# The product h*c moved to VectorE, and three smaller edits, in a conv-attention-LSTM kernel

## The chip, the cores and the metric

The kernel runs on one core of a Trainium2 chip. The metric is device microseconds of one execution. Five engines work side by side, each with its own queue in a fixed order: TensorE (PE; PEld is its weight load), VectorE (DVE), ScalarE (ACT), GpSimd (POOL), and SyncE (SP), which here issues DMAs alone.

## The reference

Eight images of 56 x 56 x 256 go through two layers, all in float32. In short:

```
x = x + conv_attn(group_norm(x))      # 7x7 regions of 64 tokens; each region attends to the 4 regions
                                      # that its pooled query ranks highest; of 256 keys the best 32
                                      # scores of each query are kept (k2 = TS // 8); plus a 3x3 depthwise
                                      # convolution of v, plus an output projection
t = x as (8, 3136, 256)
t = t + window_attn(layer_norm(t))    # each token attends to 3 neighbours on either side
xt = layer_norm(t);  h = c = 0
for step in range(3136):              # a recurrence over the tokens, 8 images at once
    i = sigmoid(xt @ U_i + b_i + h @ V_i);   g = tanh(xt @ U_c + b_c + h @ V_c)
    o = sigmoid(xt @ U_o + b_o + h @ V_o)
    c = h * c + i * g                 # the old h takes the place of a forget gate
    h = o * tanh(c)
t = t + all h
```

The product that the change moves is `h * c` in the line of the new c.

## The kernel before

**Stages.** An image is cut into 7 rows of 448 tokens (`ROW`, 7 regions of 64). A unit is one row of one image; the 56 units run row by row, and within a row over the 8 images. A unit does `queries_and_lepe` (projections and convolution), 7 times `region` (attention of one region), `project`, and `window_attention`, whose last part, `gates`, writes the terms xt @ U + b of the recurrence to DRAM (`xgd`). Ahead of that, `norm_and_route` reads each image twice: once for statistics, once for keys and values. In what follows all of this is called the bulk work.

**The recurrence** (`recurrence`, lines 1304 to 1411) can take a row's 448 tokens once all eight images have finished that row. So the tokens of row p run beside the bulk work of row p+1, and the tokens of the last row run alone, at the end. A step of the recurrence is a chain over four engines:

- `sums_of`: 24 small matmuls add h @ V to a PSUM bank (`r_sum`) that already holds the token's terms;
- ACT: tanh of the bank to `r_th` (the sigmoids are tanhs of halved arguments);
- DVE: a 32 x 32 block transpose of `r_th` into `cell`, a buffer in which the gates and the old product stand interleaved (there are two, used in turn);
- DVE: `tensor_tensor_scan` over `cell` gives the new c (`r_c`), and reads i, g and the product h*c there;
- ACT: tanh of c to `r_tc`; DVE: `scalar_tensor_tensor` of the output gate and `r_tc` gives h, in `r_hs`.

Beside the chain, ACT halves c (`r_half`, line 1375), POOL multiplies it by h into the cell of the next step (line 1377), and an empty instruction on DVE (`seen_by`, line 314) waits for that product. From token 2688 on (`APART`), the output gate has matmuls, tanh and transpose of its own, and only 16 matmuls stand in the chain.

Terms come from DRAM by `load_terms`: `XB` tokens at a time, in four DMAs each, into two buffers `r_gin`; `place` copies two tokens' terms to a PSUM bank on ACT.

**The planner.** `_Plan` records every operation with an estimate of how long it holds its engine (`held`) and when its result is there (`late`), from `_time` or `timed`; then `run` (line 369) plays all five engines forward, chooses for each engine the ready operation of the lowest rank, and so fixes the order of every queue. Operations of the recurrence have rank 0 and `chain=True`, or rank -1 for those beside it. Bulk work may start only if it ends by `until`, the time at which the chain is expected on that engine plus a slack. For DVE this is `max(20, 1.5 * (due - now))` ns past the due time (line 434). A long operation of POOL is held back in part of each step (line 438). When PE would idle for over `FILL` ns ahead of its next work, a matmul of no use (`spare`, line 641) is put in, which keeps PE busy.

**Two-operand operations on POOL.** Over 400 ns and with two tensors each are: `pe - left` in `region` (line 983, 28 in a unit), the bias of the gates (1212, 12 in a unit), the biases of `project` and `window_attention` (1056 and 1155, 4 each), and the sum of a region (1020, 7 in a unit).

**Normalisations.** `normalize` (785) works on `xn` (two operations in a unit) and on `xchunk` (`keys_values`, two in each of 56 calls); `layer_norm` (1027) on `xln`, twice for each block of 112 tokens. All are `tensor_scalar` on DVE: subtract a mean, multiply by a scale.

Of the kernel before, what the change touches and what calls it, by code (L numbers as in the profile page):

```python
# [10 lines left out]
F32 = mybir.dt.float32  # L11
# [29 lines left out]
TB = 16  # L41
XB = 8
GATES = 3
# [15 lines left out]
FAR = 10**12  # L59
FILL = 250  # L60
LONG = 400
SLACK = {"PE": 60, "DVE": 120, "ACT": 60, "POOL": 60, "SP": 1000}

# [39 lines left out]
def _time(engine, name, view, reads, args, kw):  # L103

    n = max([_count(v) for v in [view] + reads])
    if engine == "SP":
        return 650, 2400 + 9 * n // 4
    if engine == "PE":
        held = 160 if name == "transpose" else 5 * _count(view) // 3 + 110
        return held, held + 200  # L110
    if engine == "POOL":
        t = 180 + 15 * n // 7
        return (1050, 1050) if ALU.pow in args else (t + 90, t)
    if engine == "ACT":
        t = 5 * n // 7 + 100
        if kw.get("accum_out") is not None:
            return t + 150, t + 260
        if isinstance(kw.get("bias"), _View) or view.buf.banks:
            return t + 120, t + 200
        return t + 20, t + 110  # L120
    held = 25 * n // 24 + 60
    if name == "reciprocal":
        return 20 * n // 3 + 60, 20 * n // 3 + 150
    if name == "transpose":
        return held + 40, held + 120
    if name == "tensor_tensor_scan":
        return 2 * n + 80, 2 * n + 170
    if name == "match_replace":
        return held + 65, held + 150
    if name == "scalar_tensor_tensor":  # L130
        return held + 20, held + 100
    return held, held + 90
# [72 lines left out]
class _Op:  # L205
    __slots__ = (
        "engine", "trace", "held", "late", "rank", "chain", "before", "open", "due", "start",
        "takes", "pair", "made",
    )
# [24 lines left out]
class _Plan:  # L234
# [78 lines left out]

    def seen_by(self, engine, op, view):


        def trace():
            made = engine.engine.engine_nop()
            self.tc.add_manual_dep(
                made.ins, op.made[0].ins.name,  # L320
                mybir.DependencyInfo(mybir.DependencyClass.Sync, mybir.DependencyReason.DATA),
                reason="seen before it is read",
            )

        self.add(engine.name, [trace], [view], [], 10, 10)
        return self.ops[-1]

    def add(self, engine, traces, reads, writes, held, late):
        op = _Op()
        op.engine, op.trace, op.held, op.late = engine, traces, held, late  # L330
        op.rank, op.chain = self.mode
        op.rank = (op.rank, len(self.ops))
        op.before, op.takes, op.start = {}, [], None
        op.pair = engine == "DVE" and len(reads) > 1
        self.ops.append(op)
        for views, write in ((reads, False), (writes, True)):
            for v in views:
                self._depend(op, v, write)
                if v.buf.pool is not None:
                    if not v.buf.users:  # L340
                        op.takes.append(v.buf)
                    if not v.buf.users or v.buf.users[-1] is not op:
                        v.buf.users.append(op)
# [25 lines left out]
    def run(self, tc, fill):  # L369
# [35 lines left out]
        def expected(engine):  # L405
# [3 lines left out]
            for k in range(at, min(at + 7, len(chain))):  # L409
# [8 lines left out]
                if op.engine == engine or engine == "POOL" and op.pair:  # L418
                    return t
            return FAR  # L420

        filled = tied = 0
        while len(done) < len(ops) + filled:
            moved = False
            for e in engines:
# [7 lines left out]
                due = expected(e)  # L433
                until = due + (SLACK[e] if e != 'DVE' else max(20, 1.5 * (due - now)))
                for i, (rank, op) in enumerate(ready[e]):
                    if not op.chain and now + op.held > until:
                        continue
                    if e == "POOL" and op.held > LONG and (at % 6 > 3 or tied < at // 6):

                        continue  # L440
                    if any(b.free and not self._room(b, made, now) for b in op.takes):
                        continue
                    del ready[e][i]
                    op.start = now
                    free[e] = now + op.held
                    heappush(events, free[e])
                    heappush(events, now + op.late + HOP)
# [4 lines left out]
                    for b, gap in op.before.items():  # L452
                        b.due = max(b.due, now + gap)
                        b.open -= 1
                        if not b.open:
                            opened(b)
                    if op.chain:
                        at += 1
                    elif e == "POOL" and op.rank[0] == 0:
                        tied += 1  # L460
# [13 lines left out]
            if not moved:  # L474
# [4 lines left out]
                now = heappop(events)  # L479
        self.length = now  # L480
        with tc.manual_schedule():
            for op in done:
                for t in op.trace:
                    t()

    def _room(self, buf, made, now):
# [23 lines left out]
def _layers(ctx: ExitStack, tc, a, out):  # L510
# [146 lines left out]
    hss = [nc.fixed(t, (P, 2, TB, SLOT)) for t in hss]  # L657
    state = {"seen": None, "h": hss[1][:, :, TB - 1].as_of(hss[1][:, :, TB - 1, LAST:])}
    t2, xg = [], []
# [10 lines left out]
    def norm_and_route(b, im):  # L670
# [22 lines left out]
        def groups():  # L693
# [16 lines left out]
            im["rs"] = rs = images_p.tile([P, 2], F32, name="grs")  # L710
            _rsqrt(nc, rs, gm[:, 1, :], 1e-5, mhalf[:, 0:2])

        def route():
# [71 lines left out]
    def normalize(im, t):  # L785
        for k in range(2):
            nc.vector.tensor_scalar(
                t[:, k, :], t[:, k, :], im["gm"][:, 0, k : k + 1], im["rs"][:, k : k + 1],
                ALU.subtract, ALU.mult,
            )  # L790
# [109 lines left out]
    def region(qi, unit, im, row):  # L900
# [35 lines left out]
        for pair in range(groups // 2):  # L936
            both = ps_sc.tile([P, 2, 512], F32, name="sc")
            with nc.rank(0.5), nc.together(600, 800):
                for g2 in range(2):
# [86 lines left out]

    def layer_norm(i, src, mv, rs, nq=QB):

        xl = two.tile([QB, C], F32, name="xln")
        nc.vector.tensor_scalar(  # L1030
            xl[:nq], src, mv[:nq, i, 0:1], rs[:nq, i : i + 1], ALU.subtract, ALU.mult
        )
# [7 lines left out]
    def project(b, unit, im, row):  # L1040
# [30 lines left out]
        def end():  # L1071
# [3 lines left out]
            )  # L1075
            rs = small.tile([QB, NQB], F32, name="rs")
            _rsqrt(nc, rs[:, :nblk], mv[:, :nblk, 1], 1e-5, mhalf[:QB, :nblk])
            for i in range(nblk):
                nc.scalar.copy(
                    xc[:, :, LEAD + i * QB : LEAD + (i + 1) * QB],  # L1080
                    layer_norm(i, x1[:, i, :], mv, rs),
                )
# [14 lines left out]
    def window_attention(b, unit, im, row):  # L1097
# [88 lines left out]
        def begin_gates():  # L1186
            blocks = len(sizes)
            row["rs2"] = small.tile([QB, NQB + 1], F32, name="rs2")
            _rsqrt(
                nc, row["rs2"][:, :blocks], row["mv2"][:, :blocks, 1], 1e-5,  # L1190
                mhalf[:QB, :blocks],
            )
            for i, q in enumerate(sizes):
                nc.sync.dma_start(t2[t0 // QB + i][:, b, :], row["t2"][:q, i, :])

        def gates(i):
            q = sizes[i]
            xl = two.tile([P, 2, QB], F32, name="xlT")[:, :, :q]
            nc.scalar.copy(
                xl, layer_norm(i, row["t2"][:q, i, :], row["mv2"], row["rs2"], q)  # L1200
            )
# [98 lines left out]
    def blocks(t):  # L1300

        return t.rearrange("p (k g b) -> p k g b", k=2, b=nb)

    def recurrence(blk):

# [11 lines left out]
        def step(t):  # L1317
# [4 lines left out]
            now = slice(at % 2 * UJ, (at % 2 + 1) * UJ)  # L1322
            cell, after = cells[at % 2], cells[(at + 1) % 2]
            gates = cell[:, 2 : 2 + 4 * CELL].rearrange(
# [4 lines left out]
            if at < APART:  # L1329
                with nc.rank(0, chain=True):  # L1330
# [3 lines left out]
                    nc.timed(150, 190)  # L1334
                    nc.vector.transpose(gates, blocks(th))
            else:

# [18 lines left out]
            with nc.rank(0, chain=True):  # L1356
# [10 lines left out]
                nc.timed(130, 187)  # L1367
                if state["seen"]:
                    nc._edge(state["seen"], nc.ops[-2], False)
                hn = hs[:, :, t, LAST:]  # L1370
                nc.vector.scalar_tensor_tensor(hn, out_gate, 1.0, tch, ALU.add, ALU.mult)
                nc.timed(92, 161)
            state["h"] = hs[:, :, t].as_of(hn)
            half = rwork.tile([P, 2, nb], F32, name="r_half")
            nc.scalar.activation(half, c[:, :, :, 2], AF.Copy, scale=0.5)
            hc = after[:, CELL + 2 : 2 * CELL + 2].rearrange("p (k b e) -> p k b e", b=nb, e=3)
            nc.gpsimd.tensor_tensor(hc[:, :, :, 2], hn, half, ALU.mult)
            with nc.rank(-1):
                state["seen"] = nc.seen_by(nc.vector, nc.ops[-1], hc[:, :, :, 2])
            if at < APART:  # L1380
# [81 lines left out]
    for s in after(len(units) - 1):  # L1462
        s()
    made["tokens"] = SHIFTED
    follow(ready, -(-SHIFTED // TB))
# [69 lines left out]
```

## Time and profile before

| | |
|---|---|
| median of 3 runs | 9221.27 us (9216.84 to 9227.03) |
| profiled execution | 9223.24 us |
| its span | 9221.5 us |
| granted TensorE clock, mean | 0.989 |
| busy: PE, PEld | 93%, 62% |
| busy: DVE, ACT, POOL | 84%, 61%, 35% |
| first, last update of r_c | 1350.0 us, 9215.6 us |
| matmuls of no use (`spare`) | 1699.7 us |

A busy share is that of an engine over the whole span; matmuls overlap one another, so PE's is not a share of its peak. Nearly every operation is issued from one line of the recorder (L302), so groups are told apart by tile names: `r_` names belong to the recurrence. In the lists of groups, the first number behind the bar is the busy time of the group in us, the second the mean of one instruction in ns.

The run has three parts. Up to 1350 us there is bulk work alone; from there to 8300 us the bulk work and six rows of the recurrence run side by side; from 8300 us the last 451 tokens run alone.

### The profile page before, as it was taken

Reading aid. Unit: us, or ns where it says so; the run is one execution under the profiler, and the core shown is the slowest. Engines: PE = TensorE matmul, PEld = TensorE weight load, DVE = VectorE, ACT = ScalarE, POOL = GpSimd, SP = SyncE. Lnnn points to the kernel's source line nnn. Section 1 sums busy time; section 2 is a strip of 40 time slices with the busy share of each in tenths; the row PEclk is TensorE's granted clock in tenths of the full one; section 3 lists DMA queues with packets and bytes.
Section 4 is the critical chain, followed back from the end, with each engine's and each line's share of the span. In section 5 each row is a group of like instructions: output and inputs, shape, how many; then the busy total and the mean of one; then the engine's idle time right before and its main releaser. Section 6 shows DMA issues by size and latency. Waiting matters only on the chain.

```text
span 9221.5 us, 494813 instructions
## 1 busy us (share of the span) xinstructions
PE 8606.6 (93%) x200866; PEld 5694.5 (62%) x200866; DVE 7734.8 (84%) x32968; ACT 5612.8 (61%) x22855; POOL 3249.4 (35%) x7747
## 2 busy tenths in 40 slices
PE   7989989999999999999999999999999999999999
PEld 4555556666566666666656666566665666657887
DVE  6787899899999999989998899989999988864444
ACT  3555556666666666666666666666666666654444
POOL 1232343343433434333343333433334343331111
PEclk9999999999999999999999999999999999999999
DMA  6545432323323333332333323333233323220000
GB/s 198 153 130 161 112 104 79 88 79 92 89 79 88 80 90 87 81 87 77 93 82 84 89 77 89 83 87 90 78 89 81 89 75 83 76 64 25 25 24 22
DMA packets 1071250, 798.03 MB, mean 87 GB/s; under 512 B 402366, under 2 KB 1001524, under 8 KB 1068964
## 3 DMA queue, kind: packets, MB, share of 16 engines
q1 hardware_dynamic: 1068964, 766.36, 31.0%
q8 instruction: 1580, 25.89, 1.2%
q14 instruction: 706, 5.78, 0.2%
HBM read 527.08 MB, written 238.88 MB: 83 GB/s over the span
## 4 chain that ended last, share of the span: by engine, by line
DVE 50%; PE 28%; ACT 6%; issue 3%; DMA 2%; POOL 0%; SPq 0%; DVEq 0%; POOLq 0%; ACTq 0%
DVE left L302 15%; PE r_sum L302 13%; DVE top L302 13%; PE mm L302 9%; DVE r_c L302 7%; DVE r_cell L302 5%; DVE r_hs L302 4%; ACT r_th L302 2%; PE spare L641 2%; PE pt_av L302 2%; ACT r_tc L302 1%; PE sc L302 1%; DVE st L302 1%; DVE xln L302 1%; DMA xn<-xh 1%
## 5 line engine op out<-in xcount | busy, mean ns | idle before, releaser
L302 PE MATMUL r_sum<-r_v,r_hs 128*8 128x64 f32 (+2 forms) x150528 | 2715.8, 220 | 353.1 <-DVE r_hs L302 234.4
L302 PEld LDWEIGHTS r_sum<-r_v,r_hs 128*8 128x8 f32 (+2 forms) x150528 | 2180.1, 96 | 1285.8 <-DVE r_hs L302 1190.5
L302 POOL TENSOR_TENSOR r_cell<-r_hs,r_half 128x16 f32<-128x16 f32 x3136 | 714.3, 228 | 3999.7 <-DVE r_hs L302 2679.3
L302 DVE MATCH_REPLACE8 left<-top,left 128x256 f32<-128x256 f32 x4704 | 1901.9, 408 | 0.0
L302 DVE MAX8 top<-left 128x8 f32<-128x256 f32 x4704 | 1852.1, 412 | 1.9
L302 ACT ACTIVATE r_th<-r_sum 128x64 f32<-128x64 f32 x3587 | 797.9, 222 | 1679.1 <-PE r_sum L302 1633.9
L641 PE MATMUL spare<-ident 128*32 128x128 f32 x11852 | 1699.7, 277 | 9.8 <-issue 8.2
L302 DVE STREAM_TRANSPOSE r_cell<-r_th 128x64 f32<-128x64 f32 x3136 | 806.4, 257 | 864.6 <-ACT r_th L302 830.4
L302 POOL TENSOR_TENSOR pe<-pe,left 128x256 f32<-128x256 f32 x1568 | 1144.3, 733 | 898.9 <-ACT left L302 429.2
L641 PEld LDWEIGHTS spare<-ident 128*32 128x32 f32 x11852 | 1154.5, 110 | 276.6 <-issue 239.3
L302 ACT ACTIVATE r_tc<-r_c 128x16 f32<-128x16 f32 x3136 | 700.1, 223 | 838.7 <-DVE r_c L302 798.9
L302 DVE TENSOR_TENSOR_SCAN r_c<-r_cell 128x48 f32<-128x48 f32 x3136 | 892.2, 285 | 94.0
L302 ACT ACTIVATE pe<-sc,nmax 128x256 f32<-128x256 f32 x1568 | 712.6, 467 | 200.4 <-DVE left L302 134.5
L302 ACT ACTIVATE left<-left,nmax 128x256 f32<-128x256 f32 x1568 | 766.7, 503 | 15.6 <-DVE left L302 7.0
L302 PE MATMUL mm<-wu,xlT 128*112 128x256 f32 (+2 forms) x1856 | 746.8, 521 | 7.8 <-ACT xlT L302 7.0
L302 PE MATMUL pt_av<-ident,pe 128*128 128x128 f32 x3136 | 693.8, 289 | 58.2 <-ACT pts L302 19.0
L302 DVE MAX8 top<-sc 128x8 f32<-128x256 f32 x1568 | 622.5, 416 | 47.1 <-PE sc L302 43.2
L302 ACT ACTIVATE r_half<-r_c 128x16 f32<-128x16 f32 x3136 | 652.4, 208 | 0.0
L302 DVE MATCH_REPLACE8 left<-top,sc 128x256 f32<-128x256 f32 x1568 | 640.6, 412 | 0.2 <-issue 0.2
L302 ACT COPY pts<-pt_av 128x256 f32<-128x256 f32 x1568 | 570.7, 364 | 84.7 <-PE pt_av L302 77.3
L302 DVE SCALAR_TENSOR_TENSOR r_hs<-r_cell,r_tc 128x16 f32<-128x16 f32 x2685 | 547.7, 204 | 67.9 <-ACT r_tc L302 63.8
L302 ACT ACTIVATE et<-top,nmax 128x32 f32<-128x32 f32 x1568 | 497.5, 318 | 165.7 <-DVE top L302 159.1
(128 smaller groups left out, 11864.3 us busy)
## 6 DMA issues: line engine op xcount, KB each, us to landing
kg<-kd SPq DMA_DIRECT2D x1568, 64.0 KB
vg<-vd SPq DMA_DIRECT2D x1568, 64.0 KB
vshift<-lines SPq DMA_DIRECT2D x336, 232.0 KB
xgd<-gs SPq DMA_DIRECT2D x224, 336.0 KB
r_gin<-xgd SPq DMA_DIRECT2D x1568, 48.0 KB
xchunk<-xt SPq DMA_DIRECT2D x112, 448.0 KB
lines<-v SPq DMA_DIRECT2D x112, 290.0 KB
xn<-xh SPq DMA_DIRECT2D x56, 560.0 KB
```

The costliest lines, as they stand in the source:

```text
L302: made[:] = [method(*[v.real() if isinstance(v, _View) else v for v in args], **{k: v.real() if isinstance(v, _View) else v for k, v in kw ...
L641: raw.tensor.matmul(spare[:32, :P], ident[:, :32], ident, start=True, stop=True, skip_group_check=True)
```

## The change

1. **Product.** `r_half`, the POOL product and the empty DVE instruction go. A new `keep_state` does `(h * 0.5) * c` in one `scalar_tensor_tensor` on DVE. Up to token 2688 it is recorded in the chain right behind the transpose, ahead of the scan of the same step; from token 2688 on it is recorded right behind the update of h, outside the chain.
2. **POOL.** A two-operand operation of POOL over 400 ns is planned only in the first part of a step (at most 3 chain operations behind the update of h, and so that it should end 140 ns ahead of the next two-operand operation of the chain on DVE), and it is made to wait by semaphore for the latest update of h (`behind`). The planner also keeps two-operand operations of DVE and POOL apart in its model (`locked`).
3. **DVE's slack.** The factor 1.5 becomes 2.0 while the bulk work on DVE is behind the recurrence's progress, and 0.2 while it is ahead by more than 2% (`yields`).
4. **Normalisations** become ACT activations, x * rs + off, with off = -mean * rs from a small new DVE operation.
5. **Loads of terms:** `XB` is 16 in place of 8.
6. **Estimates:** other constants in `_time` for PE, ACT and POOL; `FILL` 220 in place of 250; 540 in place of 600 ns for a pair of score matmuls.

```diff
-XB = 8
+XB = 16
-FILL = 250
+AHEAD = 0.02
+FILL = 220
+CLEAR = 200
...
-        held = 160 if name == "transpose" else 5 * _count(view) // 3 + 110
-        return held, held + 200
+        held = 160 if name == "transpose" else 5 * _count(view) // 3 + 50
+        return held, held + 140
...
-        op.pair = engine == "DVE" and len(reads) > 1
+        op.closes, op.behind = False, None
+        op.pair = engine in ("DVE", "POOL") and sum(
+            not v.buf.banks and _count(v) > 8 for v in reads
+        ) > 1
...
                 if op.engine == engine or engine == "POOL" and op.pair:
-                    return t
+                    return t - (CLEAR if engine == "POOL" else 0)
...
+        beside = sum(o.chain for o in ops[:self.last])
+        work = sum(o.held for o in ops[:self.last] if o.engine == "DVE" and not o.chain)
+        begun = 0
+        def yields():
+            ahead = spent - begun - (at / beside + AHEAD) * (work - begun)
+            return 0.2 if ahead > 0 else 2.0
...
-                until = due + (SLACK[e] if e != 'DVE' else max(20, 1.5 * (due - now)))
+                until = due + (SLACK[e] if e != "DVE" else max(20, yields() * (due - now)))
...
-                    if e == "POOL" and op.held > LONG and (at % 6 > 3 or tied < at // 6):
+                    if op.pair and locked["POOL" if e == "DVE" else "DVE"] > now:
                         continue
+                    if e == "POOL" and op.pair and op.held > LONG and 0 < at < len(chain):
+                        if since > 3:
+                            continue
+                        op.behind = closed
...
+                if getattr(op, "behind", None):
+                    self.tc.add_manual_dep(
+                        op.made[0].ins, op.behind.made[0].ins.name,
...
     def normalize(im, t):
         for k in range(2):
-            nc.vector.tensor_scalar(
-                t[:, k, :], t[:, k, :], im["gm"][:, 0, k : k + 1], im["rs"][:, k : k + 1],
-                ALU.subtract, ALU.mult,
+            nc.scalar.activation(
+                t[:, k, :], t[:, k, :], AF.Identity, bias=im["off"][:, k : k + 1],
+                scale=im["rs"][:, k : k + 1],
             )
...
-        nc.vector.tensor_scalar(
-            xl[:nq], src, mv[:nq, i, 0:1], rs[:nq, i : i + 1], ALU.subtract, ALU.mult
+        nc.scalar.activation(
+            xl[:nq], src, AF.Identity, bias=off[:nq, i : i + 1], scale=rs[:nq, i : i + 1]
         )
...
+    def keep_state(cell):
+        h, c = state["past"]
+        hc = cell[:, CELL + 2 : 2 * CELL + 2].rearrange("p (k b e) -> p k b e", b=nb, e=3)
+        nc.vector.scalar_tensor_tensor(hc[:, :, :, 2], h, 0.5, c, ALU.mult, ALU.mult)
+        nc.timed(92, 150)
...
                     nc.vector.transpose(gates, blocks(th))
+                    turned = nc.ops[-1]
+                    if state["past"]:
+                        keep_state(cell)
+                        turned.before[nc.ops[-1]] = turned.held
...
-                if state["seen"]:
-                    nc._edge(state["seen"], nc.ops[-2], False)
...
+                nc.ops[-1].closes = True
             state["h"] = hs[:, :, t].as_of(hn)
-            half = rwork.tile([P, 2, nb], F32, name="r_half")
-            nc.scalar.activation(half, c[:, :, :, 2], AF.Copy, scale=0.5)
-            hc = after[:, CELL + 2 : 2 * CELL + 2].rearrange("p (k b e) -> p k b e", b=nb, e=3)
-            nc.gpsimd.tensor_tensor(hc[:, :, :, 2], hn, half, ALU.mult)
-            with nc.rank(-1):
-                state["seen"] = nc.seen_by(nc.vector, nc.ops[-1], hc[:, :, :, 2])
+            state["past"] = hn, c[:, :, :, 2]
+            if APART <= at + 1 < SHIFTED:
+                with nc.rank(-1):
+                    keep_state(cells[(at + 1) % 2])
```

## The prediction

> **What bounds the kernel now.** I read three things in this order: busy time by stretch, one step of the chain in order of time, and then the shortest, median and longest instruction of each tile that the change touches.
>
> Stretches first, whole engines (columns: length, then busy us and instructions of PE, PEld, DVE, ACT, POOL; clock; DMA share; GB/s):
>
> ```profile
> 0.00:1350.00 1350.00, 1178.39 (x8172) 682.94 (x8173) 1063.60 (x4045) 684.48 (x2065) 399.57 (x732) 0.95 0.52 143
> ...
> 4820.00:5938.00 1118.00, 1057.56 (x27541) 696.94 (x27540) 1017.51 (x4393) 731.86 (x3025) 435.17 (x1056) 1.00 0.32 85
> 5938.00:5981.00 43.00, 37.75 (x358) 20.68 (x357) 41.57 (x177) 26.66 (x91) 22.31 (x37) 1.00 0.34 90
> ...
> 8300.00:9221.00 921.00, 870.03 (x26036) 736.99 (x26034) 387.42 (x1862) 435.31 (x2255) 113.51 (x484) 1.00 0.09 24
> ```
>
> The same stretches for tile `r_tc` alone (DVE, then ACT) count steps:
>
> ```profile
> 4820.00:5938.00 1118.00, 89.46 (x448) 100.03 (x448) 1.00 0.32 85
> 5938.00:5981.00 43.00, 0.00 (x0) 0.00 (x0) 1.00 0.34 90
> ```
>
> A row's 448 steps take 1118 us, 2.496 each. Then the recurrence stands still for 43 us, while DVE is 97% busy: it waits for the next row's terms, that is, for the bulk work. Row starts near 1350, 2504, 3657, 4820, 5981, 7143 and 8300 us give a mean period of 6950 / 6 = 1158 us. DVE is busy for 1059 us of the 1161 shown: it sets the row, with some 102 us of holes. The last part, 921 us for 451 tokens, is the chain alone (2.04 us a step).
>
> One step, from h to h, in order of time (start, busy us):
>
> ```profile
> 5000.74 0.17 DVE L302 SCALAR_TENSOR_TENSOR r_hs<-r_cell,r_tc 128x16 f32<-128x16 f32 x1
> ...
> 5000.96 0.86 PE L302 MATMUL r_sum<-r_v,r_hs 128*8 128x64 f32 x48
> 5001.08 0.23 POOL L302 TENSOR_TENSOR r_cell<-r_hs,r_half 128x16 f32<-128x16 f32 x1 [2.17 <-DVE r_hs L302]
> ...
> 5001.45 0.73 POOL L302 TENSOR_TENSOR pe<-pe,left 128x256 f32<-128x256 f32 x1
> ...
> 5001.89 0.22 ACT L302 ACTIVATE r_th<-r_sum 128x64 f32<-128x64 f32 x1
> ...
> 5002.21 0.25 DVE L302 STREAM_TRANSPOSE r_cell<-r_th 128x64 f32<-128x64 f32 x1
> ...
> 5002.50 0.26 DVE L302 TENSOR_TENSOR_SCAN r_c<-r_cell 128x48 f32<-128x48 f32 x1
> ...
> 5002.79 0.22 ACT L302 ACTIVATE r_tc<-r_c 128x16 f32<-128x16 f32 x1 [0.37 <-DVE r_c L302]
> ...
> 5003.05 0.27 DVE L302 SCALAR_TENSOR_TENSOR r_hs<-r_cell,r_tc 128x16 f32<-128x16 f32 x1
> ```
>
> This undisturbed step is 2.31 us. The POOL product is done at 5001.31, 1.2 us ahead of the scan: it is not on the chain. Two steps on, `pe` starts on POOL at 5002.55 and the update of h at 5003.05 takes 0.27 in place of 0.17. The tiles show how common that is (shortest/median/longest ns):
>
> ```profile
> L302 DVE TENSOR_TENSOR_SCAN r_c<-r_cell x3136: 227/258/830, 1350.0 to 9215.6; 128x48 f32<-128x48 f32 x196
> ...
> L302 DVE SCALAR_TENSOR_TENSOR r_hs<-r_cell,r_tc x2685: 140/175/696, 1350.6 to 8252.2; 128x16 f32<-128x16 f32 x192
> ```
>
> I set every scan and update of h from 1500 to 8240 us against POOL's long operations. Of 2619 scans, 855 overlap one: 357 ns on average against 257. Of 2619 updates, 391 do: 384 against 172. Summed over the medians that is 82 + 75 = 157 us, 26 a row or 0.060 a step.
>
> **The product.** 448 a row, 2688 beside bulk work. DVE starts its next operation before the last one's time is over (the pair of MAX8 of 0.41 takes 0.74 together, so 0.08 earlier). So the product starts 0.26 - 0.08 = 0.18 after the transpose, lasts 0.175 like the update of h, which has its form, and the scan follows some 0.035 later, as it follows the transpose now (0.29 - 0.255): 0.39 against 0.29, say 0.09 to 0.10. Lower end 0.09; upper end, if the product first waits until the transpose is written, 0.25 + 0.035 + 0.175 + 0.035 - 0.29 = 0.21. I take 0.09, 40 us a row, on DVE and on the chain alike. Taken away: the empty DVE instruction (where one lies between two MATCH_REPLACE8, these start 333 in place of 326 ns apart: 3 us a row), ACT's `r_half` (0.11 of issue, on an engine 65% busy) and 0.23 of POOL: nothing on the path.
>
> **POOL's wait.** Today POOL's queue waits for h anyway, since its product stands in the queue: 2266 us in 1889 waits between 1350 and 8250 us. The new semaphore takes that wait's place, and I price it at zero. What queues behind it: `nmax`, for which ACT's exponentials wait, and `pe`, for which PE's transposes wait. If the new places work, the 26 us a row of overlap go; ends: 0 and 26. I take 26, as an operation that begins just after h and lasts 0.73 is over at 1.0, before the transpose at 1.47.
>
> The Trainium skill, "SBUF — State Buffer", section on the engine and AXI sides, says DVE with two SBUF inputs and GpSimd share one port pair under an exclusive lock, the later one being blocked in full. The 696 ns update, 521 over its median, agrees. The rule also speaks against the change: it adds a third operation a step that can be locked out. By it, each long POOL operation that is late would delay product and scan by up to 0.73.
>
> **Normalisations.** From 1350 us on there are 392 `xln` (427 to 443 ns) and 92 `xn` (584 ns): 65 x 0.355 + 15 x 0.50 = 31 us a row off DVE, counting 0.08 less each for the overlap. On ACT, by `left<-left,nmax` (128 x 256, a bias by partition, 503 ns), they cost 65 x 0.42 + 15 x 0.7, some 38 us, against 448 x 0.11 = 49 that `r_half` frees. Up to 1350 us 112 `xchunk` (592), 64 `xln` and 20 `xn` leave DVE: 57 + 23 + 10 = 90 us. There DVE is 79% busy, and 190 us of its waits are for `xchunk` DMAs, which stay; I take a third, 30 (ends 0 and 90).
>
> The Trainium skill, "ScalarE: Activation LUTs", section "Rules for kernel authors", says to multiply and add on VectorE, not ScalarE. By it the move loses per instruction, and the rows agree (503 against 435). The engine that sets the row decides here, so I don't follow it.
>
> **Loads.** 784 fewer DMA issues of SP, each of twice the bytes. DVE's waits for DMA beside the recurrence are 27.5 us, all for `xn`. Zero; ends -2 and +2 us a row for the first chunk.
>
> **Planner.** DVE waits for `r_th` for 372 us between 1350 and 8250, 62 a row. The factor 2.0 lets bulk work use part of these holes, and the chain can pay, having 43 to 48 us a row to spare. Ends: 62 gained; 20 lost, if 0.2 rules. I take 10. In the last part, the sixth `spare` pair that 220 allows takes 0.22 of PE's 0.37 idle before each h, so it costs nothing; without that cover at most 451 x 0.17 = 77 us.
>
> **Sum.** A row: +40 - 26 - 3 - 31 - 10 = -30 us, six rows -180. With -30 at the start, 9223 - 210 = 9013; the median is 2 us below the profiled execution, so 9011. The chain allows it: 448 x (2.496 + 0.09 - 0.06) = 1132 against a row of 1128.
>
> **Rivals.**
> 1. *The holes close.* With 2.0 and better estimates the wait at the row's end and DVE's holes both shrink, 62 us a row in place of 10: 9011 - 6 x 52 = 8700 at best, half of it 8855. For: every row has the wait. Against: the chain would need 1076 us a row, 2.40 a step, with the product in it.
> 2. *The locks stay*, the change doesn't do what it says: POOL's queue still runs late into scan and product. +26 a row: 9170. For: POOL has one long operation for nearly every step (48 x 8 = 384 a row for 448 steps), so few starts can be missed.
> 3. *The product becomes the bound* (slower). If it waits for the transpose to be written, 0.21 a step: 448 x (2.496 + 0.21 - 0.06) = 1185 us a row, no wait at the row's end, +27 x 6 - 30 = 9350. It decides from 0.15 a step on (43 to 48 us of spare time over 448 steps, plus 0.06). For: both write the same cell. Against: DVE writes in order, and nothing that the product reads comes from the transpose.
>
> **Numbers.** Forecast 0.53 (own range 8920 to 9090), rival 1 0.20, rival 2 0.12, rival 3 0.15. The range reaches from 8800 to 9210: it takes in the upper half of rival 1 and rival 2. About 0.2% (18 us) is what a measurement can tell from no change. Faster: 0.53 + 0.20 and most of rival 2, 0.79; same 0.05; slower 0.16.
>
> **What would show it.** Transpose to scan 0.38 to 0.39; `r_c` and `r_hs` with a mean near the median (258, 175); no 0.27 updates; row period near 1128 with a shorter standstill; 2.03 a step at the end. It would be wrong if transpose to scan is 0.5, if DVE waits for `r_th` more than now, or if `pe` is late and `top` or `left` waits on DVE.

## The result

The changed kernel takes 9263.21 us, median of 5 runs (9254.49 to 9267.22), beside 9221.27 before: a ratio of 1.0047, 95% interval 1.0035 to 1.0059, so 0.47% slower. The forecast was 9011 us.

**The profile after.** First the busy time by stretch, whole engines, the columns as before. The stretches are the start, one row, the time from VectorE's last `left` operation (the search of the last region) to the end of the rows, and the last part:

```profile
0.00:1347.00 1347.00, 1203.60 (x8371) 712.17 (x8372) 978.64 (x3867) 798.61 (x2283) 394.62 (x732) 0.95 0.51 144
4850.00:6010.00 1160.00, 1113.60 (x28271) 756.96 (x28269) 1056.60 (x4907) 739.90 (x2726) 357.27 (x638) 0.99 0.31 85
8150.00:8301.00 151.00, 146.44 (x3581) 108.33 (x3583) 64.01 (x302) 58.40 (x223) 26.54 (x40) 1.00 0.17 44
8301.00:9257.00 956.00, 954.97 (x26939) 839.17 (x26938) 464.76 (x2306) 391.01 (x1797) 11.24 (x28) 1.00 0.08 22
```

The same stretches for tile `r_tc` (DVE, then ACT), one instruction of it for each step:

```profile
4850.00:6010.00 1160.00, 80.08 (x449) 100.03 (x449) 0.99 0.31 85
8150.00:8301.00 151.00, 11.33 (x62) 13.87 (x62) 1.00 0.17 44
8301.00:9257.00 956.00, 78.76 (x449) 99.14 (x449) 1.00 0.08 22
```

Three things are to be seen. The start is 3 us shorter, though DVE has 85 us less to do there (979 in place of 1064). In the rows the standstill at a row's end is gone, yet a step takes 2.58 us on average and the six rows end where they did, near 8300 us: when VectorE has searched the last region, at 8150, the recurrence still has some 62 steps to go. And a step of the last part takes 956 / 449 = 2.13 us in place of 2.04, 41 us over the whole part, as much as the kernel lost.

The tiles of the chain (shortest/median/longest ns):

```profile
L309 DVE TENSOR_TENSOR_SCAN r_c<-r_cell x3136: 214/258/821, 1346.7 to 9256.8; 128x48 f32<-128x48 f32 x196
L309 DVE SCALAR_TENSOR_TENSOR r_cell<-r_hs,r_c x3135: 129/142/723, 1349.2 to 9255.4; 128x16 f32<-128x16 f32 x196
L309 DVE SCALAR_TENSOR_TENSOR r_hs<-r_cell,r_tc x2685: 147/175/743, 1347.2 to 8298.6; 128x16 f32<-128x16 f32 x192
```

The medians are the undisturbed times, and all three longest ones lie above 700 ns: the product on VectorE can be held up as long as the scan and the update of h.

**One account for all runs.** From the records of each trace I add up, from the first step to the end of VectorE's last `left` operation (called the end of the bulk work from here on; the last unit's projection, window attention and gates come after it), the holes of VectorE, its busy time with the chain, and its busy time with bulk work, each from one start to the next. "Steps left" are those of the six rows (2685 steps) that have not begun by then. "Overlap" is what scan, product and update of h take over their undisturbed medians between 1500 and 8240 us; nearly all of it falls beside long operations of GpSimd.

```
                      median  ratio   bulk ends  holes chain  bulk  steps left  overlap  last part/step
before                9221     1         8202      603  1560   4688      22        157       2.034
after                 9263     1.0047    8150      555  1668   4579      61        169       2.126
e1 norms back         9298     1.0082    8196      453  1659   4730      62        173       2.126
e2 product back       9157     0.9935    8050      683  1423   4594      61         91       2.121
e3 old estimates      9476     1.0274    8471      892  1727   4488       3        152       2.045
e4 factor 1.5         9359     1.0150    7860      408  1588   4517     229        206       2.124
e5 last part          9233     1.0001    8162      562  1670   4580      61        171       2.047
e6 pool free          9397     1.0176    8297      468  1911   4564      61        400       2.126
e7 product alone      9353     1.0139    8277      362  1929   4633      57        429       2.047
e8 e2 and e5          9143     0.9902    8076      707  1423   4597      61         89       2.037
e9 product after h    9297     1.0077    8164      485  1837   4496      64        242       2.124
e10 AHEAD             9254     1.0034    8189      565  1682   4590      39        not taken  2.124
e11 e8 and AHEAD      9143     0.9909    8114      720  1436   4608      39        not taken  2.035
e12 e8 and estimate   9127     0.9896    8060      741  1410   4584      61         83       2.038
```

(Median in us; all other columns in us from the profiled execution; ratios to the kernel before on the same chip, whose median was 9221 to 9232 in the four sets. So runs of different sets are compared below by their ratios, times 9221.) Before to after: bulk -109, chain +108, holes -48, so the bulk work ends 52 us earlier; the 39 more steps that are left then give it all back; the last part adds 41.

### The profile page after: what moved, and what is told of

Its sections match the earlier page's. It is cut to its first block, busy times and chain, and to the rows that moved or that the text cites. A ratio compares the mean times of both kernels' runs of the same rounds, so it can differ in the third digit from the quotient of the medians.

```text
span 9262.4 us, 491987 instructions
## 1 busy us (share of the span) xinstructions
PE 8854.8 (96%) x204338; PEld 6101.7 (66%) x204338; DVE 7756.2 (84%) x35527; ACT 5632.7 (61%) x20415; POOL 2564.5 (28%) x4611
## 4 chain that ended last, share of the span: by engine, by line
PE 60%; DVE 16%; ACT 6%; issue 2%; DMA 1%; POOL 0%; SPq 0%; ACTq 0%; POOLq 0%; DVEq 0%
PE r_sum L309 22%; PE mm L309 18%; PE spare L669 13%; DVE left L309 4%; PE pt_av L309 4%; PE sc L309 3%; DVE top L309 3%; DVE r_cell L309 3%; DVE r_c L309 3%; ACT pe L309 2%; ACT r_th L309 1%; DVE r_hs L309 1%; ACT xln L309 1%; ACT left L309 0%; DMA xn<-xh 0%
## 5 line engine op out<-in xcount | busy, mean ns | idle before, releaser
L309 PE MATMUL r_sum<-r_v,r_hs 128*16 128x64 f32 (+2 forms) x150528 | 2778.3, 220 | 210.2 <-DVE r_hs L309 144.8
L309 PEld LDWEIGHTS r_sum<-r_v,r_hs 128*8 128x8 f32 (+2 forms) x150528 | 2237.3, 96 | 960.9 <-DVE r_hs L309 818.5
L669 PE MATMUL spare<-ident 128*32 128x128 f32 x15324 | 2132.1, 277 | 2.3 <-POOL ident masks.py:199 1.5
L669 PEld LDWEIGHTS spare<-ident 128*32 128x32 f32 x15324 | 1522.8, 110 | 334.7 <-issue 278.4
L309 PE MATMUL mm<-wu,xlT 128*112 128x512 f32 (+3 forms) x1856 | 739.5, 513 | 2.6 <-ACT xlT L309 1.7
L309 PEld LDWEIGHTS pt_av<-ident,pe 128*128 128x128 f32 x3136 | 382.3, 144 | 372.0 <-issue 231.3
L309 PE MATMUL sc<-kg,q 32*64 32x256 f32 x6272 | 525.8, 404 | 33.6 <-ACT pe L309 28.9
L309 DVE SCALAR_TENSOR_TENSOR r_hs<-r_cell,r_tc 128x16 f32<-128x16 f32 x2685 | 495.7, 185 | 65.7 <-ACT r_tc L309 45.5
```

Of the source, the lines that this page charges most:

```text
L309: made[:] = [method(*[v.real() if isinstance(v, _View) else v for v in args], **{k: v.real() if isinstance(v, _View) else v for k, v in kw ...
L669: raw.tensor.matmul(spare[:32, :P], ident[:, :32], ident, start=True, stop=True, skip_group_check=True)
```

## The experiments

Three theories stood at first. V, the prediction's: VectorE's load sets the rows. C: with the product in it, the chain sets them. P: the planner's new rules and estimates hold the chain back.

**e1: normalisations back on VectorE.**

```diff
     def normalize(im, t):
-            nc.scalar.activation(
-                t[:, k, :], t[:, k, :], AF.Identity, bias=im["off"][:, k : k + 1],
-                scale=im["rs"][:, k : k + 1],
+            nc.vector.tensor_scalar(
+                t[:, k, :], t[:, k, :], im["gm"][:, 0, k : k + 1], im["rs"][:, k : k + 1],
+                ALU.subtract, ALU.mult,
...
...
-        nc.scalar.activation(
-            xl[:nq], src, AF.Identity, bias=off[:nq, i : i + 1], scale=rs[:nq, i : i + 1]
+        nc.vector.tensor_scalar(
+            xl[:nq], src, mv[:nq, i, 0:1], rs[:nq, i : i + 1], ALU.subtract, ALU.mult
```

> The changed kernel with all normalisations back on VectorE. Theory C (with the product in it, the chain of the recurrence sets the length of the six rows, and VectorE's bulk work is done some 100 us before the chain): the 31 us a row go onto an engine that has time to spare, ScalarE loses its 0.6 us operations that stand ahead of r_th and r_tc, and the time stays at 9200 to 9280. Theory V (the prediction's: VectorE's load sets the row): six rows of 31 us come back, 9430 to 9460.

9298 us, ratio 1.0082 [1.0064, 1.0099]: 35 us above the changed kernel. V falls, at least in its size; C's stretch, which ends at 9280, is missed by 18. VectorE's bulk time rose by 151 us and its holes shrank by 102: one us of load was worth about a quarter of a us, 38 of 151 by the time from the first step to the end of the bulk work, net of what ScalarE gains when the same operations leave it.

**e2: product back on ScalarE and GpSimd,** the rest as changed (`r_half` and `r_tc` with fewer buffers, for room).

```diff
-                    turned = nc.ops[-1]
-                    if state["past"]:
-                        keep_state(cell)
-                        turned.before[nc.ops[-1]] = turned.held
...
+            half = rwork.tile([P, 2, nb], F32, name="r_half", bufs=1)
+            nc.scalar.activation(half, c[:, :, :, 2], AF.Copy, scale=0.5)
+            hc = after[:, CELL + 2 : 2 * CELL + 2].rearrange("p (k b e) -> p k b e", b=nb, e=3)
+            nc.gpsimd.tensor_tensor(hc[:, :, :, 2], hn, half, ALU.mult)
+            with nc.rank(-1):
+                state["seen"] = nc.seen_by(nc.vector, nc.ops[-1], hc[:, :, :, 2])
```

> The changed kernel with the product halved on ScalarE and multiplied on GpSimd again, all else as changed. Theory C: transpose to scan falls from 0.37 to 0.29 us, 2688 x 0.08 = 215 us less chain, until the bulk work sets the end again: 9050 to 9160, and the standstill at the ends of rows is back. Theory P (the planner's new rules and estimates hold the chain back, not the product): 9220 to 9280.

9157 us, ratio 0.9935 [0.9918, 0.9951], faster than both kernels. The product on VectorE costs 106 us within the change. The time is as C had it, but the standstill that C expected is not there, and transposes and scans lie 0.34 us apart on average, 0.37 in the changed kernel, since now a MAX8 stands between them in 663 of the 2685 steps; the median is 0.30, in the changed kernel 0.345.

**e3: old estimates,** `FILL` 250, and 600 ns for a pair of score matmuls.

```diff
-FILL = 220
+FILL = 250
...
-        held = 160 if name == "transpose" else 5 * _count(view) // 3 + 50
+        held = 160 if name == "transpose" else 5 * _count(view) // 3 + 110
...
-        return (1050, 1050) if ALU.pow in args else (t, t)
+        return (1050, 1050) if ALU.pow in args else (t + 90, t)
...
-            with nc.rank(0.5), nc.together(540, 740):
+            with nc.rank(0.5), nc.together(600, 800):
```

(ScalarE's estimates likewise.)

> The changed kernel with the old estimates of PE, ScalarE and GpSimd, FILL 250 and 600 ns for a pair of score matmuls. Theory P: operations of ScalarE that stood ahead of r_th (203 us over the undisturbed 0.924 us in the rows, against 77 before) fall to under 120 us, and the last part goes from 2.126 back to 2.034 us a step (41 us): 9090 to 9180. Theory C alone: the last part's 41 us come back if its order returns, the rows stay: 9215 to 9270.

9476 us, ratio 1.0274 [1.0255, 1.0293]. Neither stretch holds this. P falls with its sign: in the rows the new estimates are worth much, for with the old ones the holes grow to 892 us and the standstill is back, longer than ever. Only the last part does as P said, 2.045 us a step. Which of the estimates makes the holes was not tried.

**e4: constant factor 1.5.**

```diff
-            return 0.2 if ahead > 0 else 2.0
+            return 1.5
```

> The changed kernel with the old constant factor 1.5 in VectorE's slack. Theory C: the factor 0.2 gives the chain VectorE at once (th to transpose 0.280 us on average, 0.344 before); with 1.5 this goes back up by 0.05 or more a step, and as the chain sets the rows the time rises by 100 us or more, to 9340 to 9420, less some 20 to 40 if the last part returns to 2.03 us a step. Theory V: bulk work that may start earlier shortens the rows: 9100 to 9220.

9359 us, ratio 1.0150 [1.0131, 1.0169], in time as C had it; but from tanh to transpose it is 0.302 us on average, 0.022 more in place of the 0.05 that C named, and the rest of the loss is spread over the other links of the chain. This run shows best why VectorE's load alone does not set the time. Its `r_tc` by stretch, the last row up to the end of the bulk work and from there to the end of the rows:

```profile
7000.00:7860.00 860.00, 62.68 (x327) 72.99 (x327) 1.00 0.31 83
7860.00:8401.00 541.00, 40.30 (x228) 50.90 (x228) 1.00 0.11 30
```

The bulk work is done 290 us earlier than with the change, with the fewest holes but one, and the kernel is slower: 228 steps are left, 2.37 us each, on an engine that has little else to do. Bulk work and chain must end together, and what either gains alone is lost.

**e5: the last part planned by the old estimates** of two ScalarE operations.

```diff
+        if t >= APART:
+            nc.timed(311, 391)
...
                     nc.scalar.activation(th, apart_of(at)[:, now], AF.Tanh)
+                    nc.timed(165, 255)
```

> The changed kernel with the old estimates of two ScalarE operations from token 2688 on alone: the copy of terms (311 ns in place of 208) and the output gate's tanh (165 in place of 74). Theory L (the last part is slower because, by the new estimates, the planner puts a copy of terms ahead of r_tc and the output gate's transpose ahead of the scan): 2.03 us a step again, 41 us less, 9215 to 9230, rows unchanged. Theory F (the sixth pair of spare matmuls delays h's matmuls): the last part stays at 2.12, 9255 to 9270.

9233 us, ratio 1.0001 [0.9992, 1.0011], where the changed kernel had 1.0047: the whole loss is gone, some 42 us by the ratios; the rows are nearly as they were (from their first step to the last part's first 6962 us, 6953 in the changed kernel), the spare matmuls stay. One step each, VectorE in order of time, of the changed kernel (start, busy us)

```profile
8803.47 0.26 DVE L309 STREAM_TRANSPOSE r_cell<-r_th 128x64 f32<-128x64 f32 x1 [0.79 <-ACT r_th L309]
8803.76 0.25 DVE L309 STREAM_TRANSPOSE r_tr<-r_th 128x64 f32<-128x64 f32 x1
8803.93 0.22 DVE L309 TENSOR_TENSOR_SCAN r_c<-r_cell 128x48 f32<-128x48 f32 x1
```

and of e5:

```profile
8801.14 0.26 DVE L309 STREAM_TRANSPOSE r_cell<-r_th 128x64 f32<-128x64 f32 x1 [0.79 <-ACT r_th L309]
8801.44 0.26 DVE L309 TENSOR_TENSOR_SCAN r_c<-r_cell 128x48 f32<-128x48 f32 x1
8801.61 0.22 DVE L309 STREAM_TRANSPOSE r_tr<-r_th 128x64 f32<-128x64 f32 x1
```

In the first, the output gate's transpose `r_tr` stands ahead of the scan and, as its tanh is not ready, holds it up: transpose to scan 0.46 in place of 0.30. The new estimate of that tanh, 164 ns until it is there, is shorter than the 220 ns that it takes. In the other steps a copy of terms stands ahead of `r_tc` on ScalarE. A step of the kernel before, then one of the changed kernel (start, busy us):

```profile
8800.60 0.26 DVE L302 TENSOR_TENSOR_SCAN r_c<-r_cell 128x48 f32<-128x48 f32 x1
8800.89 0.22 ACT L302 ACTIVATE r_tc<-r_c 128x16 f32<-128x16 f32 x1 [0.17 <-DVE r_c L302]
```

```profile
8801.68 0.26 DVE L309 TENSOR_TENSOR_SCAN r_c<-r_cell 128x48 f32<-128x48 f32 x1
8801.58 0.22 ACT L309 ACTIVATE r_th<-r_sum 128x64 f32<-128x64 f32 x1
8801.83 0.27 ACT L309 COPY r_sum<-r_gin 128x128 f32<-128x128 f32 x1
8802.04 0.22 ACT L309 ACTIVATE r_tc<-r_c 128x16 f32<-128x16 f32 x1
```

So `r_tc` follows the scan after 0.36 in place of 0.29.

**e6: GpSimd's guard taken away.**

```diff
-CLEAR = 200
+CLEAR = 0
...
-                    if op.pair and locked["POOL" if e == "DVE" else "DVE"] > now:
-                        continue
...
-                        if since > 3:
-                            continue
-                        op.behind = closed
```

> The changed kernel without the wait of GpSimd's operations for h, without the limit of 3 chain operations, without the 200 ns and without keeping the two engines apart in the plan. In the changed kernel the two-operand operations of the chain lose 169 us to overlap with GpSimd in the rows (25 update of h, 74 scan, 70 product, over their medians). Theory G (the guard works and is worth its price): the loss rises to 250 us or more and the time by 60 us or more, 9320 or above. Theory N (the guard removes nothing): a loss of 140 to 200 us and 9220 to 9290.

9397 us, ratio 1.0176 [1.0159, 1.0193]; overlap 400 us. The guard is needed: 231 us more overlap, and by the ratios some 119 us more time. It works where it holds, which is not everywhere (see the first point of the next section).

**e7: the product alone,** on the kernel before, with `keep_state` as in the change and GpSimd's old rule counted by 7 chain operations a step. The rule's other half, a long operation only once that step's product is planned (`tied`), has nothing left to count and is gone.

```diff
-                    if e == "POOL" and op.held > LONG and (at % 6 > 3 or tied < at // 6):
+                    if e == "POOL" and op.held > LONG and op.rank[0] > 0 and (at + 1) % 7 > 4:
...
                     nc.vector.transpose(gates, blocks(th))
+                    turned = nc.ops[-1]
+                    if state["past"]:
+                        keep_state(cell)
+                        turned.before[nc.ops[-1]] = turned.held
```

> The kernel before with the product on VectorE between transpose and scan as its only edit (the planner's old rule for GpSimd is kept in sense: no long operation is planned while the next chain operation is the tanh of c or the update of h). Theory C+V (product and what it meets at the shared operands lengthen the chain and load VectorE by 0.06 to 0.10 us a step, and nothing else of the change pays for it): transpose to scan 0.37 or more, 9380 to 9520. Theory H (the row's spare 43 to 48 us hide it): 9210 to 9260.

9353 us, ratio 1.0139 [1.0122, 1.0156], a little below the expected stretch. The product alone makes the kernel slower. Its tiles (shortest/median/longest ns):

```profile
L302 DVE TENSOR_TENSOR_SCAN r_c<-r_cell x3136: 231/258/1436, 1353.6 to 9345.0; 128x48 f32<-128x48 f32 x196
L302 DVE SCALAR_TENSOR_TENSOR r_cell<-r_hs,r_c x3135: 128/143/2043, 1355.9 to 9343.7; 128x16 f32<-128x16 f32 x196
L302 DVE SCALAR_TENSOR_TENSOR r_hs<-r_cell,r_tc x2685: 148/176/1711, 1354.2 to 8413.0; 128x16 f32<-128x16 f32 x192
```

The medians are unchanged, the longest scan and update of h are 1.7 and 2.5 times those of the kernel before (830 and 696). All the overlaps sum to 429 us, 157 before: with neither the product in its queue nor the half of the rule that counted it, GpSimd's waits for h ahead of that product (2266 us before) are gone, and 813 of its 1278 `pe` between 1500 and 8240 us begin over 1.0 us behind h, 659 of 1284 before.

**e8: e2 and e5 together.**

> The product back on ScalarE and GpSimd together with the old estimates of the two ScalarE operations in the last part. Theories C and L together: 9157 - 40 = 9117, between 9105 and 9130, faster than both kernels.

9143 us, ratio 0.9902 [0.9885, 0.9919], beside a median of 9232 before in this set. The two gains add within the intervals; this one holds 9117 / 9221 = 0.9887, though the median lies above the expected stretch.

**e9: the product on VectorE, but right behind the update of h,** outside the chain.

```diff
-                    turned = nc.ops[-1]
-                    if state["past"]:
-                        keep_state(cell)
-                        turned.before[nc.ops[-1]] = turned.held
...
-            if APART <= at + 1 < SHIFTED:
+            if at + 1 < SHIFTED:
```

> The changed kernel with the product on VectorE still, but in every step recorded right behind the update of h, outside the chain, where it lies beside the matmuls. Theory C (its place between transpose and scan costs, as that lengthens the chain): transpose to scan 0.29, the rows as with the product on GpSimd, 9110 to 9200. Theory V (VectorE's load of 2688 more operations costs, wherever they stand): 9240 to 9290.

9297 us, ratio 1.0077 [1.0057, 1.0096]. C falls here (V's stretch, too, ends 7 us short): the chain is shorter (the quickest steps take 2.26 us in place of 2.30) and the kernel no faster. Against e2 only the engines of the product differ, and by the ratios 131 us. The product's line, with a median of 176 and a longest of 1142, shows that it now meets GpSimd's operations, which wait for the same h:

```profile
L309 DVE SCALAR_TENSOR_TENSOR r_cell<-r_hs,r_c x3135: 152/176/1142, 1345.9 to 9269.0; 128x16 f32<-128x16 f32 x196
```

It alone loses 153 us to overlap, 70 in the changed kernel; all three 242. While it is held, VectorE's queue stands behind it: from tanh to transpose it is 0.348 us on average, 0.280 in the changed kernel. So e9 doesn't show what the product's time alone costs.

**e10: AHEAD 0.012,** and **e11,** the same on e8.

```diff
-AHEAD = 0.02
+AHEAD = 0.012
```

> The changed kernel with AHEAD 0.012 in place of 0.02. Theory B (the factor 0.2 sets in only when the bulk work leads by 2% of its load, so the chain is 64 steps behind when VectorE's bulk work ends, of which only some 42 fit into the 100 us that the last row's gates still need): 42 to 45 steps behind, the end of the six rows 20 to 40 us earlier, 9220 to 9245. Rival (the two ends move together, VectorE's load alone decides): 9255 to 9275.

> The product back on ScalarE and GpSimd, the old estimates in the last part, and AHEAD 0.012. Theory B: 10 to 25 us less than with 0.02, 9118 to 9135. Rival: 9143 as before.

e10: 9254 us, ratio 1.0034 [1.0023, 1.0044]; e11: 9143, 0.9909 [0.9892, 0.9925]. AHEAD does set the backlog, 39 steps in place of 61 in both, but the time moves by less than the intervals tell apart: inconclusive for e10, nothing for e11. In e11 the bulk work ends 38 us later than in e8 (8114 and 8076) and a standstill of some 15 us is back at the ends of the last two rows: the backlog is where the bulk work's gain goes, not something that can be had by this constant.

**e12: e8 with 95 ns more in the plan for a normalisation on ScalarE.**

```diff
+        if isinstance(kw.get("scale"), _View):
+            t += 95
```

> The product back on ScalarE and GpSimd, the old estimates in the last part, and 95 ns more in the plan for a ScalarE operation whose scale lies in a tile (the normalisations: they hold ScalarE for about 0.50 us and are planned at 0.40). Theory A (these late normalisations delay r_th and r_tc; they stand ahead of them for some 14 us beyond the undisturbed times): 5 to 20 us less, 9120 to 9140. Rival (other orders of ScalarE weigh more): 9135 to 9160.

9127 us, ratio 0.9896 [0.9879, 0.9912]. By the ratios some 6 us below e8, within both intervals, so no more than likely. Nor is it theory A's gain: by the traces the start is 25 us shorter (first step at 1323 us, 1348 in e8) and the rows are 8 us longer. It is the fastest kernel of the study, 1.0% below the kernel before.

## Why the prediction was wrong

- **The step that failed first: "If the new places work, the 26 us a row of overlap go; I take 26."** In sum none went: 157 us before, 169 after. Scan and update of h lost 99 us in place of 157, but the product, the third two-operand operation that the prediction itself named, lost 70. Rival 2, the locks stay, was right in this, at a chance of 0.12. The places work for some operations and don't exist for the others. Loss by the GpSimd operation that is overlapped, in us, from 1500 to 8240 us (only instructions that overlap one are counted, so the sums lie 5 to 16 us above those of the account):

```
                                     before  after   e2   e6   e7
pe<-pe,left and sum<-part,sum           130      2   12  250  255
gs<-gs,bu, x<-x,bo and v<-v,bv           36    176   96  155  179
```

  Only 4 of 1283 `pe` begin over 1.0 us behind h in the changed kernel, 659 of 1284 before; of 576 `gs` it is 368. The reason stands in the code: the recorder (`record`) counts as read only tiles that the plan knows, and the biases `bu`, `bo` and `bv1` are loaded before there is a plan. So to the planner `gs`, `x` and `v` are not two-operand operations: 20 of the 55 in a unit that the text on the kernel before lists. (The prediction counts 48 a unit and leaves out the sums; and the update of 0.27 us that it puts two steps on ends the very step that it shows.) The change's second point holds for `pe` and the sum alone, while the rule that it replaced held back every operation over 400 ns. First three of GpSimd's waits in the changed kernel from 1350 to 8250 us (us in total, times, longest): `pe` and the sum wait for h, `gs` waits for its own input, and no wait of `gs`, `x` or `v` for h is found. Then one case (start, busy us), a `v` that waited for its input alone, and the scan that met it:

```profile
POOL pe L309 <- DVE r_hs L309: 1533.9, 834, 6.6
...
POOL sum L309 <- DVE r_hs L309: 256.9, 123, 6.5
...
POOL gs L309 <- ACT gs L309: 102.4, 61, 7.1
```
```profile
1710.64 0.72 POOL L309 TENSOR_TENSOR v<-v,bv 118x256 f32<-118x256 f32 x1 [1.29 <-ACT v L309]
1710.66 0.82 DVE L309 TENSOR_TENSOR_SCAN r_c<-r_cell 128x48 f32<-128x48 f32 x1
```

  No run extends the rule to the biases, so what that would be worth is not shown. What overlap costs is shown roughly by e6: 231 us of it, and GpSimd's freedom in exchange, make some 119 us of time. e7 and e9 go the same way: 429 and 242 us of overlap, 9353 and 9297 us.
- **The chain's margin hung on the same term.** The prediction's check that the chain allows the gain, 1132 us a row, takes off 0.06 a step for the overlap, and at 1132 against 1128 it is already 4 us over. With nothing taken off it is 448 x (2.496 + 0.09) = 1158, the row of the kernel before; the six rows took 6953 / 6 = 1159. That the two agree this well is in part luck: the product added 0.05 a step, not 0.09, and other links of the chain grew.
- **VectorE's load counted one for one.** The prediction took -31 us a row for the normalisations, 186 in all; e1 shows 35, net of what ScalarE gains. Holes take up much of any change in load, as the profile before already hinted with 603 us of them, and the chain and the bulk work have to end together (e4).
- **The normalisations' price on ScalarE** was taken from an exponential with one operand by partition (503 ns). These have two, and took 596 ns (`xln`) and 844 (`xn`); from the tiles of the changed kernel (shortest/median/longest ns):

```profile
L309 ACT ACTIVATE xln<-x,rso,rs x224: 583/597/641, 309.5 to 8180.6; 112x256 f32<-112x256 f32 x112
```
```profile
L309 ACT ACTIVATE xn<-xn,goff,grs x112: 837/844/880, 53.3 to 7884.2; 128x560 f32<-128x560 f32 x112
```

  The Trainium skill, "ScalarE: Activation LUTs", section "What ACT_TABLE_LOAD costs", gives 186 ns + 0.833 a column and 93 for each such operand, by which an estimate is 585 and 838: these rows agree with it within 2%, and it would have been the better price. By the records of both traces, `r_th` comes 203 us later in sum in the rows than the undisturbed 0.924 us from h's first matmul, 77 before. Most of that isn't the normalisations: with them back on VectorE (e1) it is still 171.
- **The start: 30 us expected, 3 had.** VectorE's load fell by 85 us, and its holes grew by 82 (286 to 368 us, by the gaps in the records). There its load is hardly on the path, while ScalarE's busy time grew by 114 (684 to 799); by e12 the order planned for the normalisations is worth 25 us there.
- **The last part.** That a sixth pair of spare matmuls fits into PE's idle time was right: there are 5283 in the last part, and h's matmuls still start 0.06 us behind h. That the last part stays at 2.04 us was wrong: the estimates, which I had priced only through `FILL` and the factor, changed the order there (e5), and the last part took 41 us more.
- **The product's length** was too high: transpose to scan is 0.345 us in the undisturbed steps, 0.373 on average, for 0.39, as the product takes 0.142 in place of 0.175.
- **The planner's term** came out near, by luck: holes 48 us less, for 60, but not through the factor 2.0. With a constant 1.5 (e4) they are 408 us, 147 less than with the new factors, and with the old estimates (e3) 892.
- **POOL's wait at zero:** nothing speaks against it. VectorE's waits in the changed kernel from 1350 to 8150 us (us in total, times, longest):

```profile
DVE r_cell L309 <- ACT r_th L309: 332.7, 833, 4.8
...
DVE left L309 <- POOL pe L309: 1.7, 7, 0.6
```

  GpSimd waits for h ahead of `pe`, but VectorE hardly ever waits for `pe`; what it waits for is the chain.
- **Rival 3.** Its reason, the product held back until the transpose is written, did not come: the product starts 0.17 us behind the transpose, which lasts 0.26. What it forecast did come, by overlap and smaller delays in place of that wait: no standstill at the row's end, the chain ending last, a slower kernel.
- **The signs.** Of those that would show it, none came whole: scans and updates between 1500 and 8240 us take 286 and 185 ns on average (289 and 204 before), a row 1159 us, a step of the last part 2.13. Of those for being wrong, none came either: transpose to scan stays under 0.5, VectorE waits for `r_th` 372 us from 1350 to 8250 us, as before, and hardly for `pe`. None of them asked whether each long operation of GpSimd had got its new place.

In one sum over the rows: predicted -180, of it -186 normalisations, +66 product with locks and the empty instruction, -60 holes. Measured until the bulk work ends: -109 bulk, +108 chain, -48 holes, so -49; then 52 us more until the chain has done its steps.

What stays open: how the product's 106 us split between overlap and VectorE's time. By e6's rate, an estimate for the 78 us of overlap that e2 saves is 40 us; by e1's quarter, one for 2624 issues of some 0.09 us is 60. The sum fits, but no run separates the two. No run takes back the larger loads of terms alone.

## What to carry to other kernels

A two-operand operation of VectorE that met a long one of GpSimd was held up here (a scan 0.82 us in place of 0.26), so moving a small one from GpSimd to VectorE gave GpSimd another thing to block, in the chain itself. A rule holds only the operations that its condition catches: ask the trace, tile by tile, which ones it left out, above all when a rule that held all of them goes. Where two streams must end together, a load taken off the busiest engine is worth only what the other stream can follow: ask for the exchange rate, with one run that puts the load back. When a planner's estimates change, look at the order in every stretch, also where nothing else was touched.

## What the runs showed that I had not expected

- A VectorE operation of 0.17 us took up to 2.04 us (e7), and a scan up to 2.15 us (e6, by its tile's line), beside three of GpSimd's 0.73 us operations in a row.
- Not every long two-operand operation of GpSimd does it: beside `rs<-rs,mhalf` (112 x 4, 1.04 us) the changed kernel's scans take 257 ns on average, as undisturbed. Why is not shown.
- The sign of an edit can turn between stretches: the new estimates are worth 230 us in the rows (6953 us from the first step to the first of the last part, 7183 with the old ones) and cost some 36 in the last part (e3, e5).
